# Singles, pairs and the last step: how collected steps are finished in a sequence-and-experts kernel

## The chip, the cores and the metric

The kernel runs on one core of a Trainium2 chip. The metric is the device time of the program in microseconds (us), lower is better; each version is run several times and the median counts. The core has a matrix engine (TensorE, PE in the profile; PEld is its weight load), a vector engine (VectorE, DVE), a scalar engine (ScalarE, ACT), a general engine (GpSimd, POOL) that here mostly issues gathers and scatters, and a queue engine (SyncE, SP) that only issues transfers. ACT and POOL issue transfers too; 16 DMA engines carry them all.

## The reference, cut to what matters

Two sequences (B = 2) of 4096 tokens of width 512 go through two blocks, each followed by a layer normalization of input plus result.

```python
# first block: a matrix W that learns from token to token
pred = W @ k + b;  g = 2.0 / d_h * (pred - v)
W = W - LR * outer(g, k);  b = b - LR * g;  out = W @ q + b
x = layernorm(x + out)
# second block: a shared expert, and 2 of 8 routed experts per token
shared = silu(X @ sW1 + sb1) @ sW2 + sb2
logits = einsum('btd,ed->bte', X, routing_W) + expert_bias
top_vals, top_idx = top_k(sqrt(softplus(logits)), 2)
routed = sum over the two chosen experts e: top_val * (silu(X @ rW1[e] + rb1[e]) @ rW2[e] + rb2[e])
x = layernorm(x + shared + routed)
```

## The kernel before, in words

**Tiling.** The 4096 tokens are cut into 32 chunks of P = 128 tokens; a step `c` (0 to 31) handles chunk `c` of both sequences. The first block is a recurrence over these steps (`step`, with `prep` and `invert` preparing the next one). The second block follows each step one behind (`shared`, which calls `router`). `router` ranks the 8 experts of each token, marks the `chosen` ones (rank 0 or 1), and counts by small matmuls (`pq`) at which place of its expert's list each token goes; POOL scatters the token's number to that place.

**Routed experts.** Steps 0 to 22 are group a, steps 23 to 30 group b; step 31 is done densely. When a group's tokens are all ranked (`plan`), `routed` runs over tiles of 128 tokens of one expert: gather tokens (`g`) and weights (`wb`), multiply, write the tile's rows to memory (`ge`). Group a's tiles run beside steps 24 to 27 of the recurrence, group b's behind the recurrence.

**Collecting.** `collect` brings a group's steps together again, one collected step `j` after the other: load the step's base rows (`acc`, 512 KB, a pool of 4 buffers; the last two steps of group b are still kept on chip as `x`), gather four z tiles (2 sequences x 2 experts, 2 buffers each), add each z with its weight (L956 on DVE), take mean and variance, then normalize and write to the output (`finish`). `fetch(j + 1)` issues the transfers of the next step a little at a time while step `j` is added. With `squares` on, ACT sums the squares into a z tile that has been used (L965), and ACT scales (L927); with it off, DVE takes the statistics (L970, L971) and scales (L930).

**finish.** It takes a small DVE operation on the variance (L915 or L917), a square root on ACT (L918), a reciprocal on DVE (L920, then L922), and for each sequence a scale, then the output transfer on ACT's queue (L932). It is a generator: its first piece ends behind the square root, and each further piece is the scale and output of one step. Steps are finished in pairs (`p = j % 2`): the square root is taken once for two steps, and the pieces are run from inside the next steps, ahead of the products named in `finish_at`.

**Order.** PE and DVE run in the order of the program text; that order comes from `interleave`, which always advances the part whose done share of its stated amount is smallest (a `yield` gives the amount done). ACT's and POOL's orders are laid by the framework. Group a is collected in parts: beside steps 28 to 31 with amounts 16, 16, 16 and 8 (about 3.5, 4, 4 and 2 collected steps), the rest beside group b's tiles and the shared work of step 31. Group b is collected beside the dense work of step 31 (`dense`: for each expert `pd` matmuls, Silu on ACT, `pyd` matmuls, added to x by L721 on DVE; at the end layer normalization and output).

Of the kernel before, what the change touches and what calls it, by code (L numbers as in the profile page):

```python
# [42 lines left out]
BF16 = mybir.dt.bfloat16  # L43
I32 = mybir.dt.int32
AF = mybir.ActivationFunctionType
ALU = mybir.AluOpType
AX = mybir.AxisListType

P = 128
# [5 lines left out]
K = 2  # L55
# [51 lines left out]
def postln_block(ctx: ExitStack, tc: tile.TileContext, x, xT, thK, thV, thQ, w0, b0, masks, blk,  # L107
                 unit, order, rw, eb, w1s, b1s, w2s, b2s, b2e, wcat, out):
    nc = tc.nc
    B, S, D = x.shape  # L110
    NCH = S // P
    DC = D // P
    E = rw.shape[1]
# [20 lines left out]
    sm = ctx.enter_context(tc.tile_pool(name="sm", bufs=2))  # L134
# [137 lines left out]
    groups, of_step = [], {}  # L272
# [239 lines left out]
    def router(c, lg):  # L512
        def small(tag, shape=(P, B, E), bufs=1):
            return sm.tile(list(shape), F32, tag=tag, name=f"{tag}_{c}", bufs=bufs)


        u = small("u")
        nc.vector.scalar_tensor_tensor(u, lg, -1.0, lg, ALU.mult, ALU.min)
        nc.scalar.activation(u, u, AF.Exp)
        yield  # L520
        w = small("w")
        nc.vector.tensor_scalar(w, u, 1.0, None, ALU.add)
        lnw = small("lnw")
        nc.scalar.activation(lnw, w, AF.Ln)

        rank = small("rank")
        full = [P, B, E, E]
        other = lg[:, :, None, :].broadcast_to(full)
        own = lg[:, :, :, None].broadcast_to(full)
        gt = small("gt", full)  # L530
        nc.vector.tensor_tensor(gt, other, own, ALU.is_gt)
        eq = small("eq", full)
        nc.vector.tensor_tensor(eq, other, own, ALU.is_equal)
        nc.vector.tensor_tensor(eq, eq, lower[:, None].broadcast_to(full), ALU.mult)
        nc.vector.tensor_tensor(gt, gt, eq, ALU.add)
        nc.vector.tensor_reduce(rank, gt, AX.X, ALU.add)
        yield
        wm = small("wm")
        nc.vector.tensor_scalar(wm, w, -1.0, None, ALU.add)
        z = small("z")  # L540
        nc.vector.tensor_scalar(z, wm, 0.0, None, ALU.is_equal)
        nc.vector.tensor_tensor(lnw, lnw, z, ALU.add)
        nc.vector.tensor_tensor(wm, wm, z, ALU.add)
        nc.vector.reciprocal(wm, wm)
        nc.vector.tensor_tensor(lnw, lnw, wm, ALU.mult)
        nc.vector.tensor_tensor(lnw, lnw, u, ALU.mult)
        act = small("act")
        nc.vector.scalar_tensor_tensor(act, lg, 0.0, lnw, ALU.max, ALU.add)
        nc.scalar.activation(act, act, AF.Sqrt)
        if c not in of_step:  # L550

            nc.vector.scalar_tensor_tensor(act, rank, K - 0.5, act, ALU.is_lt, ALU.mult)
            yield act
            return

        gr = of_step[c]
        j = c - gr.c0
        chosen = sm.tile([P, B, E], BF16, tag="chosen", name=f"chosen_{c}")
        nc.vector.tensor_scalar(chosen, rank, K - 0.5, None, ALU.is_lt)
        sel = small("sel", (P, B, K, E))  # L560
        full = [P, B, K, E]
        nc.vector.tensor_tensor(sel, rank[:, :, None, :].broadcast_to(full),
                                kk[:, None, :, :].broadcast_to(full), ALU.is_equal)
        yield

        ps = ps_f.tile([P, 2, B, E], F32, tag="pf", name=f"pq_{c}")
        for s in range(B):
            nc.tensor.matmul(ps[:, 0, s], before, chosen[:, s], start=True, stop=(s == 0))
            for r in range(s):
                nc.tensor.matmul(ps[:, 0, s], ones16, chosen[:, r], start=False,  # L570
                                 stop=(r == s - 1))
        for s in range(B):
            nc.tensor.matmul(ps[:, 1, 0], ones16, chosen[:, s], start=(s == 0),
                             stop=(s == B - 1))
        yield
        place = small("place")
        nc.vector.tensor_tensor(place, ps[:, 0],
                                gr.next[:, None, :].broadcast_to([P, B, E]), ALU.add)
        nc.vector.tensor_tensor(gr.next, ps[:, 1, 0], gr.next, ALU.add)
        for what, to in ((place, gr.row), (act, gr.cw)):  # L580
            v = small("selv", (P, B, K, E))
            nc.vector.tensor_tensor(v, sel, what[:, :, None, :].broadcast_to(full), ALU.mult)
            nc.vector.tensor_reduce(to[:, j], v, AX.X, ALU.add)
        ri = sm.tile([P, B, K], I32, tag="ri", name=f"ri_{c}")
        nc.vector.tensor_copy(ri, gr.row[:, j])  # L585
        for s in range(B):
            for k in range(K):
                nc.gpsimd.indirect_dma_start(  # L588
                    out=gr.tables[s * K + k],
                    out_offset=bass.IndirectOffsetOnAxis(ap=ri[:, s, k:k + 1], axis=0),  # L590
                    in_=code[:, j * B + s:j * B + s + 1], in_offset=None,
                    bounds_check=E * gr.cap - 1, oob_is_err=False)
# [287 lines left out]
                weights(k + NW)  # L880
            yield 2.0

    squares, finish_at = [True], [(2, 3)]

    def collect(gr):

# [22 lines left out]
                    z.append(t)  # L909
                    yield  # L910

        def finish(parts, mean, var, on_scalar):

            if on_scalar:
                nc.vector.tensor_scalar(var, var, 1.0 / D, EPS, ALU.mult, ALU.add)  # L915
            else:
                nc.vector.tensor_scalar(var, var, EPS, None, ALU.add)  # L917
            nc.scalar.activation(var, var, AF.Sqrt)  # L918
            yield
            nc.vector.reciprocal(var, var)  # L920
            if on_scalar:
                nc.vector.tensor_tensor(mean, mean, var, ALU.mult)  # L922
            for p, (c, acc) in enumerate(parts):
                for s in range(B):
                    m, v = mean[:, p, s:s + 1], var[:, p, s:s + 1]
                    if on_scalar:
                        nc.scalar.activation(acc[:, s, :], acc[:, s, :], AF.Identity,  # L927
                                             bias=m, scale=v)
                    else:
                        nc.vector.tensor_scalar(acc[:, s, :], acc[:, s, :], m, v,  # L930
                                                ALU.subtract, ALU.mult)
                nc.scalar.dma_start(out=out[:, c * P:(c + 1) * P, :].rearrange("s p d -> p s d"),  # L932
                                    in_=acc)
                yield

        for _ in fetch(0):
            pass
        yield 2.0
        done = iter(())
        for j in range(gr.n):  # L940
            c = gr.c0 + j
            ahead = fetch(j + 1)
            acc, z = got.pop(j)
            p = j % 2
            if p == 0:
                on_scalar, parts = squares[0], []
                two = sm.tile([P, 2, 2, B], F32, tag="fmv", name=f"fmv_{c}")
            mv = two[:, :, p]
            mean, var = mv[:, 0], mv[:, 1]
            parts.append((c, acc))  # L950

            for i in range(B * K):
                s, k = i // K, i % K
                if i in finish_at[0]:
                    next(done, None)
                nc.vector.scalar_tensor_tensor(  # L956
                    acc[:, s, :], z[i], gr.cw[:, j, s, k:k + 1], acc[:, s, :], ALU.mult, ALU.add,
                    accum_out=mean[:, s:s + 1] if on_scalar and k == K - 1 else None)
                next(ahead, None)
                yield 0.9  # L960
            if on_scalar:

                nc.vector.tensor_scalar(mean, mean, -1.0 / D, None, ALU.mult)
                for s in range(B):
                    nc.scalar.activation(z[s * K], acc[:, s, :], AF.Square,  # L965
                                         bias=mean[:, s:s + 1], accum_out=var[:, s:s + 1])
            else:
                for s in range(B):
                    st = sm.tile([P, 6], F32, tag="fst", name=f"fst_{c}_{s}")
                    nc.vector.bn_stats(st, acc[:, s, :])  # L970
                    nc.vector.bn_aggr(mv[:, :, s], st)  # L971
            if p == 1 or j == gr.n - 1:
                for _ in done:
                    pass
                done = finish(parts, two[:, 0, 0:p + 1], two[:, 1, 0:p + 1], on_scalar)
            yield 0.4
        for _ in done:
            pass
# [32 lines left out]
        if c == NCH - 2:  # L1011
            dense_weights(2)
    dense_weights(1 + B + 2)
    squares[0], finish_at[0] = False, (1, 3)
    interleave([(b.tiles * TILE, tiles[1]), (60.0, shared(NCH - 1)),
                ((a.n - sum(COLLECTED.values())) * COLLECT, collects[0])])
    squares[0] = True
    dense_weights(E - len(dense_w))
    interleave([(DENSE, dense(NCH - 1)), (b.n * COLLECT, collects[1])])


def _masks(np):
# [66 lines left out]
```

## Time and profile before

| what | us |
|---|---|
| median of 3 runs | 2638.32 |
| lowest and highest | 2638.26, 2647.33 |
| the profiled execution | 2633.89 |
| its span | 2632.1 |
| square roots of finishing (L918) | 16 passes, 0.205 each |
| table loads ahead of them | 9, 1.283 each |
| scales on ACT (L927), on DVE (L930) | 0.80, 0.54 each |
| gathers of z (L905), POOL's part | 1.01 each |

The profile is one execution. A timeline row gives start and length in us, the engine, the line of the kernel, the operation, what it writes and reads, and in brackets how long the engine stood idle just before it and what ended that wait. `x6` means that six such instructions were merged. `ACTq` and `SPq` are the issue of transfers, not their landing.

### The profile page before, as it was taken

To read this page: it belongs to the slowest core of one execution; us is meant where nothing else is said; L and a number is where in the kernel's file an instruction comes from. 1 tells how busy PE (TensorE), PEld (TensorE's weight loads), DVE (VectorE), ACT (ScalarE), POOL (GpSimd) and SP (SyncE) were. 2 spreads that over 40 slices of the span, in tenths; PEclk is the share of its full clock that TensorE was granted. 3 is DMA by queue.
4 is the path that set the end of the run, shared out by engine and by line. 5 is a ranking of instruction groups with operands and counts; after the bars stand their busy time and mean duration, and the time that the engine had idled before them with its cause. 6 is when DMAs were issued, how large, how long until landed. Compare 5 with 4: busy or idle time off the path is not lost.

```text
span 2632.1 us, 30914 instructions
## 1 busy us (share of the span) xinstructions
PE 2541.5 (97%) x10289; PEld 1642.1 (62%) x10289; DVE 1363.9 (52%) x3993; ACT 723.8 (27%) x1453; POOL 935.0 (36%) x796
## 2 busy tenths in 40 slices
PE   8999999999999999999999999999999999889897
PEld 6666666666666666666665676666767655446664
DVE  2566665565666655666666224223242466553345
ACT  1222222222222222222221232322323233334236
POOL 0223232223232322232324333333333334446654
PEclk9999999999999999999999999999999999989998
DMA  5122222222222222222223343353433456667777
GB/s 185 48 80 59 74 58 66 69 58 58 67 71 74 58 64 71 58 58 63 76 80 130 123 96 105 122 141 109 113 109 109 113 126 169 186 208 224 268 237 245
DMA packets 257647, 291.36 MB, mean 111 GB/s; under 512 B 158269, under 2 KB 171805, under 8 KB 253905
## 3 DMA queue, kind: packets, MB, share of 16 engines
q1 hardware_dynamic: 200624, 165.72, 22.1%
q0 software_dynamic: 48432, 107.42, 14.5%
q10 hardware_dynamic: 8432, 16.25, 1.6%
q8 instruction: 82, 1.34, 0.2%
q14 instruction: 77, 0.62, 0.1%
HBM read 344.38 MB, written 99.65 MB: 169 GB/s over the span
## 4 chain that ended last, share of the span: by engine, by line
PE 85%; issue 5%; DMA 4%; DVE 3%; POOL 2%; ACT 1%; SPq 0%; POOLq 0%; ACTq 0%; DVEq 0%
PE pkq L330 16%; PE pye L857 8%; PE po L449 8%; PE pr L433 8%; PE pr L438 8%; PE phe L846 8%; PE pw L493 8%; PE ph L621 4%; PE py L661 4%; PE pa L343 4%; PE pe L475 2%; PE po L487 2%; PE pg L837 2%; PE pz L414 2%; DMA wb<-wcat_in,widx 1%
## 5 line engine op out<-in xcount | busy, mean ns | idle before, releaser
L375 DVE SCALAR_TENSOR_TENSOR X<-L,X 128x31 f32<-128x31 f32 (+22 forms) x1472 | 409.0, 327 | 27.5 <-DMA L<-dL 10.5
L846 PEld LDWEIGHTS phe<-gT,wb 128*128 128x128 f32 x2208 | 269.7, 194 | 61.9 <-issue 58.9
L588 POOL DMA_INDIRECT gt<-code,ri x124 | 127.3, 1027 | 504.0 <-DVE ri L585 475.4
L860 DVE TENSOR_TENSOR o<-pye,wb 128x512 f32<-128x512 f32 x138 | 95.4, 692 | 400.8 <-PE pye L857 390.0
L857 PE MATMUL pye<-wb,he 128*128 128x512 f32 x552 | 268.7, 609 | 18.8 <-ACT he L850 11.9
L846 PE MATMUL phe<-gT,wb 128*128 128x128 f32 x2208 | 272.9, 277 | 7.0 <-DMA wb<-wcat_in,widx 5.6
L493 PE MATMUL pw<-R,K 128*128 128x512 f32 x496 | 240.6, 608 | 12.7 <-DVE x L488 7.9
L330 PE MATMUL pkq<-xT,thK 128*128 128x256 f32 x1024 | 242.8, 381 | 7.2 <-DMA thK<-thK_in 7.2
L828 POOL DMA_INDIRECT wb<-wcat_in,widx x138 | 144.8, 1049 | 286.2 <-DVE o L860 158.4
L330 PE MATMUL pkq<-xT,thQ 128*128 128x256 f32 x1024 | 244.9, 383 | 1.0 <-DVE Z L416 1.0
L330 PEld LDWEIGHTS pkq<-xT,thK 128*128 128x128 f32 x1024 | 195.0, 191 | 80.1 <-issue 59.3
L449 PE MATMUL po<-W,kq 128*128 128x512 f32 x512 | 242.6, 596 | 1.0 <-DVE K L471 1.0
L433 PE MATMUL pr<-thV,xT 128*128 128x512 f32 x512 | 240.7, 593 | 0.0
L438 PE MATMUL pr<-W,kq 128*128 128x512 f32 x512 | 240.2, 592 | 0.0
L330 PEld LDWEIGHTS pkq<-xT,thQ 128*128 128x128 f32 x1024 | 190.2, 191 | 46.9 <-issue 24.9
L483 POOL PARTITION_ALL_REDUCE ar<-R x23 | 141.6, 6158 | 206.4 <-issue 186.7
L850 ACT ACTIVATE he<-phe,wb 128x128 f32<-128x128 f32 x276 | 86.6, 364 | 436.5 <-PE phe L846 376.9
L337 ACT COPY kq<-pkq 128x256 f32<-128x256 f32 x256 | 82.8, 375 | 433.2 <-PE pkq L330 433.2
L494 DVE TENSOR_TENSOR W<-pw,W 128x512 f32<-128x512 f32 x248 | 168.5, 689 | 63.3 <-PE pw L493 59.6
L822 POOL DMA_INDIRECT g<-gy,gidx x138 | 139.8, 1013 | 153.4 <-PE pg L837 120.7
L493 PEld LDWEIGHTS pw<-R,K 128*128 128x128 f32 x496 | 91.4, 192 | 136.3 <-issue 97.8
L857 PEld LDWEIGHTS pye<-wb,he 128*128 128x128 f32 x552 | 98.5, 190 | 124.8 <-issue 90.8
(214 smaller groups left out, 3394.9 us busy)
## 6 DMA issues: line engine op xcount, KB each, us to landing
ge<-o SPq DMA_DIRECT2D x138, 256.0 KB
xT<-xT_in SPq DMA_DIRECT2D x32, 512.0 KB
x<-x_in SPq DMA_DIRECT2D x32, 512.0 KB
L<-dL SPq DMA_DIRECT2D x128, 128.0 KB
gy<-x SPq DMA_DIRECT2D x31, 512.0 KB
gb<-x SPq DMA_DIRECT2D x29, 512.0 KB
y_out<-acc ACTq DMA_DIRECT2D x29, 512.0 KB
dT_K<-kq SPq DMA_DIRECT2D x92, 128.0 KB
```

What stands on the lines that cost most here:

```text
L330: nc.tensor.matmul(ps[:, i].rearrange("p s t -> p (s t)"), th[:, dc, (ec + i) * P:(ec + i + 1) * P], xt[:, dc].rearrange("p s t -> p (s t) ...
L375: nc.vector.scalar_tensor_tensor(X[:, h, j + 1:], L[:, j + 1:, j], X[:, h, j:j + 1], X[:, h, j + 1:], ALU.mult, ALU.add)
L433: nc.tensor.matmul(ps, xt[:, dc, s, :], nthV_sb[:, dc, :], start=(dc == 0), stop=False)
L438: nc.tensor.matmul(ps, KQ[:, ec, s, 0, :], W[s][:, ec, :], start=False, stop=(ec == DC - 1))
L449: nc.tensor.matmul(ps, KQ[:, ec, s, 1, :], W[s][:, ec, :], start=(ec == 0), stop=False)
L483: nc.gpsimd.partition_all_reduce(ar, R, P, bass_isa.ReduceOp.add)
L493: nc.tensor.matmul(ps, K[s][:, ec, :], F[s], start=True, stop=True)
L494: nc.vector.tensor_tensor(W[s][:, ec, :], ps, W[s][:, ec, :], ALU.add)
L822: nc.gpsimd.indirect_dma_start(out=g_t[k], out_offset=None, in_=gr.y, in_offset=bass.IndirectOffsetOnAxis(ap=gr.gidx[:, k:k + 1], axis=0), ...
L828: nc.gpsimd.indirect_dma_start(out=wbuf[k % NW], out_offset=None, in_=wcat, in_offset=bass.IndirectOffsetOnAxis(ap=gr.widx[:, k:k + 1], ax ...
L846: nc.tensor.matmul(ps[:, hc, :], w[:, dc * HF + hc * P:dc * HF + (hc + 1) * P], t[:, dc, :], start=(dc == 0), stop=(dc == DC - 1))
L857: nc.tensor.matmul(ps, h[:, hc, :], w[:, O2 + hc * D:O2 + (hc + 1) * D], start=(hc == 0), stop=(hc == HC - 1))
```

## The change

It has four parts. Collected steps are finished in pairs only once `paired` is set, which happens behind the recurrence; before that each step is finished alone, and so are the last two steps of each group. The very last collected step is scaled half on DVE and half on ACT, with one output transfer on SP's and one on ACT's queue. `chosen` is computed right behind `rank` and no longer behind the activation's chain. The stated amount of group b's collecting is 1.1 times what it was.

```diff
@@ router
         nc.vector.tensor_reduce(rank, gt, AX.X, ALU.add)
+        if c in of_step:
+            chosen = sm.tile([P, B, E], BF16, tag="chosen", name=f"chosen_{c}")
+            nc.vector.tensor_scalar(chosen, rank, K - 0.5, None, ALU.is_lt)
         yield
...
         j = c - gr.c0
-        chosen = sm.tile([P, B, E], BF16, tag="chosen", name=f"chosen_{c}")
-        nc.vector.tensor_scalar(chosen, rank, K - 0.5, None, ALU.is_lt)
         sel = small("sel", (P, B, K, E))
@@ collect
-    squares, finish_at = [True], [(2, 3)]
+    squares, finish_at, paired = [True], [(2, 3)], [False]
...
-        def finish(parts, mean, var, on_scalar):
+        def finish(parts, mean, var, on_scalar, final):
...
                     m, v = mean[:, p, s:s + 1], var[:, p, s:s + 1]
-                    if on_scalar:
+                    if final and s == 0:
+
+                        nc.vector.tensor_scalar(acc[:, s, :], acc[:, s, :], v, m,
+                                                ALU.mult, ALU.add)
+                        nc.sync.dma_start(out=out[s, c * P:(c + 1) * P, :], in_=acc[:, s, :])
+                    elif on_scalar:
...
-                nc.scalar.dma_start(out=out[:, c * P:(c + 1) * P, :].rearrange("s p d -> p s d"),
-                                    in_=acc)
+                if final:
+                    nc.scalar.dma_start(out=out[1, c * P:(c + 1) * P, :], in_=acc[:, 1, :])
+                else:
+                    nc.scalar.dma_start(
+                        out=out[:, c * P:(c + 1) * P, :].rearrange("s p d -> p s d"), in_=acc)
...
-        done = iter(())
+        done, parts = iter(()), []
...
-            p = j % 2
+            p = 0 if len(parts) != 1 else 1
             if p == 0:
-                on_scalar, parts = squares[0], []
+                on_scalar = squares[0]
...
-            if p == 1 or j == gr.n - 1:
+            if p == 1 or not paired[0] or j >= gr.n - 2:
                 for _ in done:
                     pass
-                done = finish(parts, two[:, 0, 0:p + 1], two[:, 1, 0:p + 1], on_scalar)
+                done = finish(parts, two[:, 0, 0:p + 1], two[:, 1, 0:p + 1], on_scalar,
+                              gr is groups[-1] and j == gr.n - 1)
+                parts = []
@@ behind the recurrence
-    squares[0], finish_at[0] = False, (1, 3)
+    squares[0], finish_at[0], paired[0] = False, (1, 3), True
...
-    interleave([(DENSE, dense(NCH - 1)), (b.n * COLLECT, collects[1])])
+    interleave([(DENSE, dense(NCH - 1)), (1.1 * b.n * COLLECT, collects[1])])
```

## The prediction, made before the changed kernel ran

> **What bounds the kernel now.** I read the page first. TensorE is busy nearly all the time, so an edit pays only where PE stands still or in the stretch behind its last matmul.
>
> ```profile
> PE 2541.5 (97%) x10289; PEld 1642.1 (62%) x10289; DVE 1363.9 (52%) x3993; ACT 723.8 (27%) x1453; POOL 935.0 (36%) x796
> ```
>
> Collecting begins in step 28, so I then took the busy time of each engine over steps 28, 29 and 30 (from one step's first `pr` matmul to the next).
>
> ```profile
> 2094.21:2158.82 64.61, 62.30 (x223) 37.91 (x222) 45.40 (x140) 20.09 (x42) 30.43 (x30) 1.00 0.51 116
> 2158.82:2224.45 65.63, 62.56 (x223) 38.06 (x222) 44.84 (x146) 24.22 (x51) 29.25 (x29) 1.00 0.64 170
> 2224.45:2298.89 74.44, 64.58 (x222) 38.91 (x221) 44.89 (x146) 24.21 (x51) 29.19 (x29) 0.93 0.69 198
> ```
>
> Columns: stretch, length, busy us of PE, PEld, DVE, ACT, POOL, granted clock, DMA share, GB/s. Step 30 has the work of step 29 and takes 8.8 us more, at a clock of 0.93. The timeline shows why:
>
> ```profile
> 2264.67 0.38 ACTq L932 DMA_DIRECT2D y_out<-acc  x1
> ...
> 2269.63 0.75 POOL L898 DMA_DIRECT2D acc<-gb  x1 [0.31 <-issue]
> ...
> 2281.26 0.75 DVE L956 SCALAR_TENSOR_TENSOR acc<-z,cw,acc 128x512 f32<-128x512 f32 x1 [8.47 <-DMA acc<-gb]
> ...
> 2286.11 5.21 PE L493 MATMUL pw<-R,K 128*128 128x512 f32 x6 [7.91 <-DVE x L488]
> ```
>
> I count the L956 rows: 2281.26 is the first product of collected step 11. Its base rows `acc` use the buffer of step 7 (four buffers). Step 7 is the second of pair (6,7), so it is scaled only inside step 9, at 2263.84, and written at 2264.67; POOL can issue the load at 2269.63, and it lands at 2281.24. DVE, in program order, stands 8.47 us, with the eviction L488 behind it; PE stands 7.91 us. Its next six `pw` matmuls take 5.21 us, the clock being 0.70 from 2285 to 2295.
>
> Last the end of the run:
>
> ```profile
> 2603.90 1.02 POOL L905 DMA_INDIRECT z<-ge,sidx  x1 [0.30 <-issue]
> ...
> 2609.11 0.79 DVE L956 SCALAR_TENSOR_TENSOR x<-z,cw,x 128x512 f32<-128x512 f32 x1 [4.23 <-DMA z<-ge,sidx]
> ...
> 2612.23 2.84 PE L718 MATMUL pyd<-wb,hd 128*128 128x512 f32 x6 [1.62 <-ACT hd L710]
> ...
> 2614.28 0.74 DVE L721 SCALAR_TENSOR_TENSOR x<-pyd,act,x 128x512 f32<-128x512 f32 x1
> ...
> 2628.12 0.38 ACTq L932 DMA_DIRECT2D y_out<-x  x1
> ```
>
> PE ends near 2615; 17 us of DVE, ACT and output follow, up to 2632.1.
>
> **Singles in the recurrence.** Walking the yields, steps 0 to 12 now finish one by one, (13,14) to (19,20) in pairs, 21 and 22 alone. The output of step 7 then leaves at the last product of step 8: the scale that now stands at 2254.58 (step 6's) becomes step 7's, with its write at 2256.1 instead of 2264.67. The write took about 4.4 us until POOL was released (2264.67 to 2269.1), so the load can go near 2261 and has 11.8 us until DVE wants it at 2272.8, against 11.6 measured. The stall goes. What is late next: the gathers of step 11, issued at 2267.01 and 2268.31 in the same queue ahead of that load, so landed before 2281. Bounds for step 30: 4 us if they hold DVE, 9.8 if it falls to step 28's 64.61. I take step 29's length, nearest because it has the same finishes: **-8.8**. Step 29 has a smaller such wait (1.7 us on `acc`) and is 1.0 longer than step 28: **-1.0** (0 to -1.0).
>
> Added: sqrt passes rise from 16 to 24, seven of them here, each with three small DVE rows (0.16, 0.17, 0.16). 7 x 0.5 = 3.5 us over four steps in which DVE has some 20 us idle per step: nothing. The new wait is L920 on ACT's sqrt; queued behind it is the step's last product, then evictions. The sqrt falls between the products at 2263.38 and 2264.68, where ACT does `act`'s sqrt at 2263.72 anyway; if that cover is gone it costs one table load, 1.28.
>
> A rule speaks against this part. The sqrt's table loads number 9 in 16 passes, the first at 2369.3: none inside the recurrence, and a load takes 1283 ns. The Trainium skill, ScalarE: Activation LUTs, "What ACT_TABLE_LOAD costs", puts a switch at that plus about 1.38 us of drain, 2.66 in all. Seven passes, there and back, would by it be 37 us of ACT; by the rows 0 to 18. The rows also show no drain (load 2563.76 + 1.28, sqrt at 2565.05), so I take them. ACT idles 41 us per step: even the rule's price would meet PE only if it held a `kq` copy beyond the 6.51 us that such copies wait for PE.
>
> **Chosen behind the ranks.** PE waits for `chosen` twice only: 3.00 us at 1400.03 and 2.90 at 2317.98. At the first, ranks end at 1398.24; `chosen` takes 0.17, so `pq` starts near 1398.5: -1.5, and nothing else holds the `pkq` matmuls behind it. At the second, ranks end at 2314.9, but the `py` matmuls behind `pq` need the second Silu, which ends at 2318.42: only -0.5. **-2.0**, bounds 0 and -5.9. No other queue is touched.
>
> **Behind the recurrence.** PE waits 5.13 us for the first routed tokens, issued 2343.08, with DMA share 1.01 from 2349 to 2361. Two 0.5 MB outputs (2344.68, 2349.02) are in flight; one of them now leaves in step 31 before. 0.5 MB at the 402 GB/s of that stretch is 1.3 us; by halves between queues **-0.7** (0 to -1.4). The tile loop has six sqrt passes before and after: nothing.
>
> **The final stage.** With 1.1 the collecting is placed before more of the dense work: the last dense half is now behind everything that collecting does on DVE. The stage runs in rounds of two steps: z lands, products, squares (which give z free), gather, landing. Rounds, by first products of steps 0, 2, 4, 6: 14.1, 15.5, 13.1 us. Now one dense eviction less (0.7) stands in each: three rounds, step 6 starts 2.1 earlier. Behind it: products of step 6 with two dense evictions, 4.9; ACT's scales (1.6) and squares (1.8) until L915, 7.5; two more scales, a table load and the sqrt, 10.6; last product, eviction and first layernorm, 14.2; ACT scale, squares and small rows, 17.8; DVE scale 0.55, last eviction, layernorm and ACT scale, 21.8; output 3.0: 24.8, against 23.0 now (2609.11 to 2632.1). 1.8 - 2.1 = **-0.3**. Bounds: -4 if ACT takes the sqrts first, +5 if each of its passes queues behind scales.
>
> The output price: two 0.5 MB writes end 4.0 us after the last issue. The skill's DMA: Bandwidth & Descriptors, "Anatomy of one DMA", has 2.0 us fixed plus bytes at 436 GB/s, 2.6 for 0.25 MB. Halving the row's moved part from about 2 us to 1 gives 3.0; by the rule the sum would be 0.4 better.
>
> **The sum.** -8.8 - 1.0 - 2.0 - 0.7 - 0.3 = -12.8 us. The profiled execution ran 2633.89 (span 2632.1), and would run 2621.1; the median of the runs is 4.4 above it, so I forecast 2638.3 - 12.8 = **2625.5**.
>
> **Rivals.**
> - *The next transfer is late.* The gathers of step 11 hold DVE for half the stall. For: DMA share 0.97 from 2265 to 2275. Against: they stand ahead of the load. Step 30 gains 4: -8.0 in all, 2630.
> - *Everything helps.* Step 30 falls to 64.61 (-9.8), `chosen` gives 4 because the clock's dip behind the wait goes too (eight `pkq` at 1400.16 take 3.59 us, at 1407.02 1.89), tail -4, tokens -1.4, step 29 -1.0: -20, 2618. For: the clock rows. Against: ACT has 15 us of work in the last 20.
> - *The final stage turns against it: slower.* DVE now waits for z ahead of evictions for which PE needs a bank. If gathers land like the base load, in 11.6 us instead of 4.5, a round is 4.4 + 2.5 + 11.6 = 18.5 us; step 6 starts at 2566.4 + 55.5 = 2621.9, 12.8 late, and with the 1.8 of the tail and -12.5 elsewhere this gives +2.1: 2640. It decides from rounds of about 18 us; the longest now is 15.5. For: DMA share near 0.9 there; against: no round came near.
>
> **Chances.** Forecast 0.45, late transfer 0.21, everything 0.22, final stage 0.12. Differences below 0.5% are about what a measurement of this kernel can't tell from none; faster by more is below 2625.1. Just under half of the forecast's share (0.22), all of the third case and 0.02 of the second lie there: 0.46. Slower by more (above 2651.5) takes 0.10: most of the last case, since longer landings have no upper row. 0.44 is left. Forecast's own range 2621 to 2631; with the others 2614 to 2641.
>
> **What would show it.** Right: step 30 near 65 us at clock 1.00, no wait of DVE on `acc<-gb` over 2 us; `pq` without a wait at the first place and a wait on the Silu at the second; 24 sqrt passes; a final 0.25 MB output. Wrong: DVE held in step 30 by `z`, or PE held in the dense stage by L721.

## The result, and the profile after

| | us, or ratio to the kernel before |
|---|---|
| before, median of 20 runs | 2635.48 |
| after, median of 20 runs | 2643.90 |
| ratio, 95% interval | 1.0026 [1.0017, 1.0034] |
| after again, 12 runs beside 35 of before | 1.0019 [1.0008, 1.0030] |
| profiled execution of after, its span | 2636.67, 2634.9 |

The forecast was 2625.5, 12.8 below the median of before that the prediction had (2638.3, three runs; twenty give 2635.48). The change made the kernel 0.2 to 0.3% slower. That is inside the 0.5% which the prediction called no difference, but with twenty runs a side it is told from none, and it has the other sign. The profiled execution of after is a quick one, 7.2 us under the median of its runs.

The same windows as before, steps 28, 29 and 30 of after (stretch, length, busy us of PE, PEld, DVE, ACT, POOL, clock, DMA share, GB/s):

```profile
2094.70:2160.20 65.50, 62.55 (x222) 37.99 (x221) 46.84 (x144) 20.20 (x44) 30.21 (x30) 1.00 0.50 121
2160.20:2225.90 65.70, 62.61 (x223) 38.11 (x222) 43.94 (x152) 24.78 (x53) 29.75 (x29) 1.00 0.56 172
2225.90:2293.70 67.80, 62.53 (x222) 38.04 (x221) 43.33 (x152) 24.60 (x53) 27.51 (x28) 1.00 0.66 204
```

Step 30 is 6.6 us shorter by these windows (6.8 by the exact cuts below) and its clock is whole again: in this execution the stall is nearly gone. The time must be lost later. I cut each execution at the first `pr` of steps 30 and 31, at the first `pg` (group b's first tile), at the first `pd` (dense work) and at the end of the span:

| version (profiled us) | step 30 | step 31 to first tile | tile loop | rest |
|---|---|---|---|---|
| before (2633.89) | 74.6 | 56.0 | 203.1 | 74.2 |
| after (2636.67) | 67.8 | 57.8 | 209.5 | 73.9 |
| after again (2651.66, highest of its runs) | 73.1 | 60.4 | 214.0 | 74.0 |

The first execution of after against before: -6.8, +1.8, +6.4 and -0.3, with +1.6 up to step 30 (0.9 of it in step 28). The sum, 2.8 with rounding, is the difference of the two profiled times. The gain is made in step 30 and lost in the tile loop, in which I had counted no change.

The timeline of after shows where PE waits there. First POOL in step 31, and the PE row that needs its work (`pc` turns the gathered `codes` into the numbers of the tokens):

```profile
2331.83 0.76 POOL L899 DMA_DIRECT2D acc<-gb  x1 [7.02 <-DMA y_out<-acc]
2332.90 0.99 POOL L769 DMA_INDIRECT codes<-gt,r  x1 [0.30 <-issue]
...
2340.95 2.52 PE L811 MATMUL pc<-ident,codes 39*128 39x39 f32 x8 [7.74 <-DMA codes<-gt,r]
```

The base load of collected step 14 needs the buffer of step 10, whose output has not landed. POOL stands 7 us at it, and the four `codes` gathers, which need nothing from it, stand behind. In before this load came behind `codes`, `wb` and `g` and stood 9.5 us with no `codes` gather behind it:

```profile
2337.73 0.96 POOL L768 DMA_INDIRECT codes<-gt,r  x1 [0.30 <-issue]
...
2357.73 0.76 POOL L898 DMA_DIRECT2D acc<-gb  x1 [9.52 <-DMA y_out<-acc]
```

Second, in the tile loop of after (`phe` are the first matmuls of a tile with its expert's weights `wb`):

```profile
2411.38 1.04 POOL L829 DMA_INDIRECT wb<-wcat_in,widx  x1 [3.51 <-issue]
2412.46 0.38 ACTq L941 DMA_DIRECT2D y_out<-acc  x1
...
2421.05 3.44 PE L847 MATMUL phe<-gT,wb 128*128 128x128 f32 x16 [2.10 <-DMA wb<-wcat_in,widx]
...
2423.70 0.75 POOL L899 DMA_DIRECT2D acc<-gb  x1 [8.64 <-DMA y_out<-acc]
2424.75 1.05 POOL L829 DMA_INDIRECT wb<-wcat_in,widx  x1 [0.30 <-issue]
...
2428.13 2.02 PE L847 MATMUL phe<-gT,wb 128*128 128x128 f32 x16 [1.20 <-DMA wb<-wcat_in,widx]
```

Again a base load (step 17) waits for an output, 8.64 us, with weight gathers behind it, and PE waits for `wb` twice. Only the second of these waits can come from the held load. The gather for which the `phe` at 2421.05 wait was issued at 2411.38, ahead of it, and landed more than nine us later; why it took so long was not tested. Behind this wait the sixteen `phe` take 3.44 us instead of 2.02. The waits of PE in the tile loop of before (2343 to 2558, first two rows) and of after (2340 to 2560): total, times, longest.

```profile
PE phe L846 <- DMA wb<-wcat_in,widx: 5.6, 4, 2.4
PE pg L837 <- DMA g<-gy,gidx: 5.1, 1, 5.1
...
PE phe L847 <- DMA wb<-wcat_in,widx: 13.3, 7, 3.3
PE pc L811 <- DMA codes<-gt,r: 7.7, 1, 7.7
```

The wait for `codes` stands mostly in place of the wait for the first tokens `g`; the waits for weights are 7.7 us more.

### The profile page after: what moved, and what is told of

It is laid out like the page before. It is cut to its first block, busy times and chain, and to the rows that moved or that the text cites. A ratio compares the mean times of both kernels' runs of the same rounds, so it can differ in the third digit from the quotient of the medians.

```text
span 2634.9 us, 30962 instructions
## 1 busy us (share of the span) xinstructions
PE 2541.3 (96%) x10289; PEld 1642.4 (62%) x10289; DVE 1362.7 (52%) x4015; ACT 726.9 (28%) x1466; POOL 933.8 (35%) x796
## 5 line engine op out<-in xcount | busy, mean ns | idle before, releaser
L330 PEld LDWEIGHTS pkq<-xT,thK 128*128 128x128 f32 x1024 | 195.2, 192 | 80.4 <-issue 59.6
```

The lines of the kernel that those rows point to most:

```text
L330: nc.tensor.matmul(ps[:, i].rearrange("p s t -> p (s t)"), th[:, dc, (ec + i) * P:(ec + i + 1) * P], xt[:, dc].rearrange("p s t -> p (s t) ...
```

## The experiments

Each ratio is to the kernel before, run beside that version, with its 95% interval. There before took 2635 to 2638 us, but 2650 beside h1_sync14, h_cut12, i_e1_sync and i_bef_sync, so their stage times are compared among themselves first. Each version has 11 or 12 runs (e2_singles and k3_late 6, m1_before_late 5), and the stage times are of one execution. Theory A took several forms; each expectation says which.

### One part at a time

*e1_chosen*: before, `chosen` moved. *e2_singles*: before, singles in the recurrence. *e3_final*: before, only the final stage (last two steps of group b alone, last step split, 1.1). *e4_ten*: the changed kernel, with singles only up to step 9.

```diff
# e1_chosen is the router part of the change alone
# e2_singles: the changed kernel, chosen put back, amount b.n * COLLECT, never final
-            if p == 1 or not paired[0] or j >= gr.n - 2:
+            if p == 1 or not paired[0] or j == gr.n - 1:
# e3_final: the changed kernel, chosen put back
-    squares, finish_at, paired = [True], [(2, 3)], [False]
+    squares, finish_at, paired = [True], [(2, 3)], [True]
-            if p == 1 or not paired[0] or j >= gr.n - 2:
+            if p == 1 or j >= gr.n - 2 + (gr is not groups[-1]):
# e4_ten, against the changed kernel
-            if p == 1 or not paired[0] or j >= gr.n - 2:
+            if p == 1 or (not paired[0] and j < 10) or j >= gr.n - 2:
```

> Only the marking of the chosen experts is moved; all else is the kernel before. Theory A (POOL's order): no change of POOL's order by this part, so 0 to -2 us against the kernel before; pq without a wait in step 24, and py waiting for the Silu in step 31 instead. Rival B (the final stage costs): the same. Rival C (the marking itself disturbs DVE's order): slower by 3 us or more.

> Only the single finishing of collected steps in the recurrence; marking, last two steps, the split of the last step and the 1.1 are as before. Theory A: the whole loss is here. Step 30 is 6 to 7 us shorter, step 31 with the plan about 6 longer (POOL stands 5 us or more on a load of base rows ahead of the gathers of codes, PE waits 5 us or more for codes), the tile loop about 6 longer; in all +3 to +9 us against the kernel before. Rival B: -6 us, since only step 30's gain is left.

> Only the final stage: the last two steps of group b single, the last one split over two engines, the amount times 1.1; marking and recurrence as before. Theory A: 0 (-2 to +2 us), the stage behind the last tile 74 us as before. Rival B: +5 us or more, PE held by L721 or by the Silu in the dense stage.

> The changed kernel, but single finishing only up to collected step 9; from step 10 on pairs as before, so that POOL's order at the plan and in the tile loop is that of the kernel before. Theory A: step 30 keeps its 6 to 7 us, codes come without a wait of PE, the tile loop is as long as before: -5 to -9 us against the kernel before. Rival B: the loss of the final stage stays, so 0 to +5 us against the kernel before.

| | ratio | step 30 | step 31 to first tile | tile loop | rest |
|---|---|---|---|---|---|
| e1_chosen | 1.0019 [1.0008, 1.0030] | 78.4 | 56.4 | 201.7 | 76.2 |
| e2_singles | 1.0051 [1.0034, 1.0067] | 71.1 | 61.6 | 212.7 | 75.7 |
| e3_final | 0.9997 [0.9987, 1.0008] | 73.0 | 59.6 | 197.8 | 77.0 |
| e4_ten | 0.9982 [0.9969, 0.9995] | 71.0 | 56.0 | 198.2 | 76.9 |
| e4_ten again | 0.9983 [0.9973, 0.9994] | 70.8 | 54.7 | 198.7 | 77.5 |

Singles cause the loss, and in step 31 and the tile loop. Three singles fewer turn the change into a gain. Two surprises: `chosen` alone costs time, in steps 29 (68.1 for 65.6) and 30; and the singles alone lose more than the whole change does. The second I cannot explain.

### Why moving chosen alone cost time

With `chosen` moved, the planner (the part of the framework that lays the orders of ACT and POOL) orders ACT differently at two places: an output (steps 3 and 7) comes behind a sum of squares instead of ahead of it, and POOL's next base load one gather later. Nothing else moves but DVE's small operations. The timeline of e1_chosen, in step 30:

```profile
2268.67 0.33 SPq L691 DMA_DIRECT2D thQ<-wcat_in  x1
2268.87 0.38 ACTq L933 DMA_DIRECT2D y_out<-acc  x1
2270.43 0.33 SPq L691 DMA_DIRECT2D wd<-wcat_in  x1
...
2282.35 0.75 POOL L899 DMA_DIRECT2D acc<-gb  x1 [8.86 <-DMA y_out<-acc]
...
2288.12 0.75 DVE L957 SCALAR_TENSOR_TENSOR acc<-z,cw,acc 128x512 f32<-128x512 f32 x1 [12.39 <-DMA acc<-gb]
```

In before this output was issued at 2264.67 and had landed some 4.4 us later. Here it goes 0.2 us behind a 1 MB weight load, and POOL sees it landed only at 2282, 13 us later. Two runs send the outputs of steps 3 and 7 from SP's queue, which gives POOL's order of before back:

```diff
-                nc.scalar.dma_start(out=out[:, c * P:(c + 1) * P, :].rearrange(...
+                (nc.sync if c in (3, 7) else nc.scalar).dma_start(out=out[:, c * P:(c + 1) * P, :].rearrange(...
```

> Chosen moved alone, as in the run that was 5.8 slower than before, but the outputs of collected steps 3 and 7 are issued on SP's queue, so that they no longer stand behind a sum of squares on ACT; POOL's order is then that of the kernel before. Theory A (moving chosen cost time only because the planner put these two outputs and with them two base loads one place later): steps 29 and 30 fall from 68.1 and 78.4 to 65.6 and at most 74.6, whole time 2633 to 2635, no slower than before. Rival C (chosen's new place itself delays DVE or PE): steps 29 and 30 stay above 67 and 77, whole time about 2640.

> Control: the kernel before with the outputs of collected steps 3 and 7 issued on SP's queue, chosen where it was. Both theories: within 3 us of the kernel before (2632 to 2638), step 30 between 70 and 75; the difference between this and the run with chosen moved is then what chosen itself does, 0 to -2 by my sum.

Measured: with `chosen` moved 0.9988 [0.9976, 1.0000], the control 0.9993 [0.9981, 1.0005]. Steps 29 and 30 of the first are 65.3 and 73.9. So the cost was the place of two outputs, and `chosen` itself is worth some 0.05%, 1.3 us, with intervals that overlap. A second pair says the same from e4_ten, taking its `chosen` back:

> Singles up to collected step 9 and the final stage as in the changed kernel, chosen where it was before. POOL's order is the same as with chosen moved, ACT's differs in one copy. Theory A (chosen alone gives 0 to 2 us where the outputs keep their places): 0 to 2 us slower than the same version with chosen moved, ratio to before 0.998 to 0.9995. Rival C (chosen's place costs time of itself): faster than that version by 2 us or more, ratio below 0.9978.

0.9994 [0.9981, 1.0007], against 0.9982 and 0.9983 with `chosen` moved: 3 us by the middle values, with intervals that overlap. `chosen` gives between nothing and 3 us.

### What costs time in step 31 and the tile loop

```diff
# h1_sync14: the changed kernel; j_after_14_17: "j in (14, 17)"
-                queue = nc.sync if gr is groups[-1] else nc.gpsimd
+                queue = nc.sync if gr is groups[-1] or j == 14 else nc.gpsimd
# h_cut12: singles up to step 11; h_cut11: up to 10; h_cut14: up to 13
+            if p == 1 or (not paired[0] and j < 12) or j >= gr.n - 2:
# j_cut12_14: h_cut12 with the first edit
```

> The changed kernel with one instruction moved: the base load of collected step 14, which waits for an output ahead of the four codes gathers on POOL, is issued on SP's queue; every other engine's order stays. Theory A (the loss is the codes gathers held behind that waiting load): the 7.7 us wait of pc on codes falls to about 3, the piece of step 31 behind its first pr falls from 57.8 to 56, and the tile loop from 209.5 towards 200, since its first weights and tokens start earlier; whole time about 2634, 9 below the changed kernel. Rival B (the loss is the other order of weight and token gathers inside the tile loop, laid by the planner): only the 2 us in step 31 go, the tile loop stays at 208 or more, whole time about 2641.

> The changed kernel with singles up to collected step 11 and pairs from 12 on: step 10 is still finished alone, so the waiting load of step 14 stands ahead of codes as in the changed kernel, but the order of gathers inside the tile loop is that of the faster version with singles up to step 9. Theory A (held codes): slow, about 2641 to 2644, tile loop 207 or more. Rival B (order in the tile loop): fast, about 2632, tile loop about 199, with only 2 us lost in step 31.

> The changed kernel once more, beside the three that follow, since times of different calls differ by more than the effects asked for. All theories: 1.0017 to 1.0034 of the kernel before.

> The changed kernel with two base loads on SP's queue: that of collected step 14 (it holds the four codes gathers) and that of step 17 (it stood 8.64 us on POOL at 2423.70 with the weight gathers of the next routed tiles behind it); all other orders are those of the changed kernel. Theory A (the loss is POOL held by base loads that wait for an output): the tiles that began at 2421 and 2428 no longer take 6.5 and 7.0 us but 4.2 to 4.8, the time falls 5 to 9 us below the changed kernel, ratio to before 0.9990 to 1.0005. Rival B (the order of the gathers themselves, or DMA engines that are full): the tiles stay slow or others get slow, the time stays within 2 us of the changed kernel. Rival D (SP's stores of expert rows are held by the moved load and with them the tile loop): slower than the changed kernel.

> Singles up to collected step 11 (pairs even-odd in the tile loop, as before) with the base load of step 14 on SP's queue, so that it doesn't hold codes. Theory A: step 30 stays near 68, the piece of step 31 ahead of the first tile falls by 2 to 5 us, and the whole is the fastest so far, ratio to before 0.996 to 0.998. Rival B: no faster than the version with singles up to step 9, ratio 0.998 or more.

> The changed kernel with step 13 finished alone too, so that the pairs behind the recurrence are (14,15), (16,17), (18,19), (20,21). Theory E (the pairing odd-even is what costs in the tile loop): tiles 10 and 11 of group b take 4.2 and 4.8 us again, the tile loop under 205, ratio to before 0.997 to 0.9995. Rival F (the more steps are finished alone, the later the tile loop): as the changed kernel or slower, ratio 1.0015 or more.

> The changed kernel with singles only up to step 10, so that the pairs are (11,12), (13,14) and so on, odd-even as in the changed kernel. Theory E: slow, tiles 10 and 11 take 6 to 7 us, ratio 1.001 to 1.003. Rival F: between the versions with singles up to 9 and 11, ratio 0.998 to 0.999.

A tile's length is the distance between first `phe` matmuls (tiles counted from 0):

| version | singles up to | ratio | step 31 to first tile | tile loop | tiles 10, 11 |
|---|---|---|---|---|---|
| before | none | 1 | 56.0 | 203.1 | 4.2, 4.8 |
| e4_ten | 9 | 0.9982 | 56.0 | 198.2 | 4.2, 4.8 |
| h_cut11 | 10 | 1.0018 [1.0006, 1.0030] | 60.4 | 208.2 | 6.8, 7.0 |
| h_cut12 | 11 | 0.9979 [0.9965, 0.9994] | 57.8 | 208.9 | 4.2, 4.8 |
| j_cut12_14 | 11 | 0.9992 [0.9980, 1.0004] | 59.9 | 204.6 | 4.2, 4.8 |
| after | 12 | 1.0026 | 57.8 | 209.5 | 6.5, 7.1 |
| h1_sync14 | 12 | 1.0003 [0.9988, 1.0018] | 60.2 | 215.2 | 6.7, 7.0 |
| j_after_14_17 | 12 | 1.0013 [1.0002, 1.0023] | 61.2 | 211.3 | 5.8, 4.3 |
| h_cut14 | 13 | 1.0016 [0.9998, 1.0033] | 61.0 | 209.5 | 6.9, 4.3 |

The tile loops have to be read with one correction. In five of the twenty executions (before, h_cut12, h1_sync14, i_e1_sync, i_bef_sync) ACT starts a Silu of the loop 2.4 to 4.5 us behind the end of its matmuls, once to three times, and the profile names no instruction or transfer of the kernel as what ended its wait (`remote`). Before, and h_cut12:

```profile
2498.80 0.63 ACT L850 ACTIVATE he<-phe,wb 128x128 f32<-128x128 f32 x2 [5.83 <-remote]
...
2497.61 0.63 ACT L851 ACTIVATE he<-phe,wb 128x128 f32<-128x128 f32 x2 [7.32 <-remote]
```

In before tile 26 is 8.7 us long with this, in h_cut12 10.4, and tile 14 there 7.4; in e4_ten, which has no such row, both take 4.2. Without it, an estimate from these tile lengths, the loop of before would be some 199 us, and that of h_cut12 too. With these two and the fifteen executions that have no such row, the loops go with the ratios: 198 to 205 us for no singles and for singles up to 9 and 11, and 208 to 214 for 10, 12 and 13. So the change costs the loop about 11 us, more than the 6.4 of the first two executions.

The `codes` gathers are not shown to be the main loss. In h_cut12 POOL waits 6.89 us ahead of them, and it is fast; taking that wait away in j_cut12_14 gave nothing that can be seen. In h1_sync14 the wait of `pc` falls to 0.7, but PE waits 9.18 us for the first token gather instead, and the tile loop, with three late Silus in it, cannot be told from that of the changed kernel. Its ratio is 0.2% under that of the changed kernel, so the wait may cost something; j_after_14_17, which has the same edit and one more, doesn't repeat that size. The second held load is real in the trace but small: with the load of step 17 off POOL, tile 11 falls from 7.0 to 4.3 as expected, tile 10 from 6.9 to 5.8 only, and tile 12 rises from 4.3 to 5.5. Some 2.5 of 5 us come back; the time falls by 0.06%, which is within the noise. That tile 10 stays slow fits the rows of after: the gather for which PE waits at its end was issued ahead of the load. In j_after_14_17 PE waits 1.41 us for that gather, with no held load on POOL.

Singles up to 10 and up to 12 give the slow tiles, up to 9 and 11 don't, so I took odd-even pairs for the cause. That falls with h_cut14, which pairs even-odd and has a slow tile 10 and a loop of 209.5. What is shown is narrower: which gathers and loads stand ahead of which on POOL differs with each cut, and the ratio does not go with the number of singles.

### What made the stall of step 30

In after, DVE waits at the same place for something else, and PE behind it:

```profile
2263.30 0.75 POOL L899 DMA_DIRECT2D acc<-gb  x1 [0.62 <-ACT z L974]
...
2278.04 0.75 DVE L965 SCALAR_TENSOR_TENSOR acc<-z,cw,acc 128x512 f32<-128x512 f32 x1 [3.42 <-DMA z<-ge,sidx]
...
2283.13 3.04 PE L493 MATMUL pw<-R,K 128*128 128x512 f32 x6 [3.08 <-DVE x L488]
```

And in the second execution of after:

```profile
2283.47 0.75 DVE L965 SCALAR_TENSOR_TENSOR acc<-z,cw,acc 128x512 f32<-128x512 f32 x1 [6.05 <-DMA z<-ge,sidx]
...
2288.39 5.49 PE L493 MATMUL pw<-R,K 128*128 128x512 f32 x6 [5.54 <-DVE x L488]
```

The base load has come, the `z` gathers haven't, and the wait differs from execution to execution. Over four executions with the changed order up to here (after, after again, h1_sync14, j_after_14_17) step 30 took 67.8, 73.1, 69.1 and 71.0, 4.3 less than before on average. All twelve with the early output and the weight loads in place took 66.9 to 73.7, 70.1 on average; four with the output where before has it (before, e3_final, i_e1_sync, i_bef_sync) took 73.0 to 74.6, 73.7 on average. So the early output is worth some 4 us. I suspected what all these transfers share. Two 1 MB loads of dense weights are issued here too; in the timeline of before:

```profile
2265.74 0.33 SPq L690 DMA_DIRECT2D thQ<-wcat_in  x1
2267.50 0.33 SPq L690 DMA_DIRECT2D wd<-wcat_in  x1
```

They are wanted only behind the tile loop. A one-column write by DVE, which the load overwrites, holds each back to the end of step 30 or 31; beside these two small rows of DVE only SP's order changes. *k3_late* has it on e4_ten, *m1_before_late* on before (pairs, `chosen` and final stage as they were), *m2_after_late* on the changed kernel.

```diff
+            if e in (1, 5):
+                nc.vector.memset(t[:, 0:1], 0.0)
             nc.sync.dma_start(out=t, in_=wcat[e * P:(e + 1) * P, 0:OB1])
```

> Singles up to collected step 9, else the changed kernel, and two of the 1 MB loads of dense weights wait for a one-column write of DVE at the end of step 30 and of step 31, so that they are no longer issued at 2268 and 2270 beside the z gathers and outputs of step 30. Theory A (these loads make z late): DVE's wait for z in step 30 falls from 5.2 to under 2 us, step 30 from 71 to 66 to 67, ratio to before 0.9965 to 0.998. Rival B (z is late because of the outputs and base loads of collecting itself): step 30 stays at 69 or more, ratio 0.998 or more.

> The kernel before, with the two 1 MB weight loads held back to the end of step 30 and of step 31 as in the fastest version; pairs as before. Theory A (the loads made the stall): the base load issued near 2269.6 lands in about 5 us instead of 11.6, DVE's wait on it falls from 8.5 to under 3 us, step 30 from 74.6 to 66 to 69, ratio to before 0.996 to 0.998. Rival G (the late output of step 7 made it, as predicted): step 30 stays above 72, ratio above 0.9985.

> The changed kernel with the same two loads held back. Theory A: step 30 at 66 to 67, but the tile loop keeps its slow tiles 10 and 11, so that it loses to the version with singles up to step 9 and held-back loads (0.9945) by 6 to 10 us: ratio to before 0.997 to 1.000. Rival H (the slow tiles too come from these loads): as fast as that version, below 0.996.

| | median | ratio | step 30 | step 31 to first tile | tile loop | rest |
|---|---|---|---|---|---|---|
| k3_late | 2625.16 | 0.9945 [0.9926, 0.9965] | 66.5 | 56.8 | 203.3 | 74.6 |
| m1_before_late | 2624.74 | 0.9962 [0.9949, 0.9976] | 65.6 | 54.7 | 198.9 | 75.0 |
| m2_after_late | 2636.17 | 1.0005 [0.9996, 1.0014] | 65.7 | 56.0 | 210.2 | 74.6 |

The window of step 30 and the timeline of m1_before_late:

```profile
2224.19:2289.78 65.59, 62.56 (x222) 38.08 (x222) 44.68 (x146) 24.21 (x51) 29.71 (x29) 1.00 0.65 177
```

```profile
2264.46 0.38 ACTq L934 DMA_DIRECT2D y_out<-acc  x1
...
2269.49 0.75 POOL L900 DMA_DIRECT2D acc<-gb  x1 [0.17 <-issue]
...
2274.00 0.75 DVE L958 SCALAR_TENSOR_TENSOR acc<-z,cw,acc 128x512 f32<-128x512 f32 x1 [1.30 <-DMA acc<-gb]
...
2279.18 3.04 PE L493 MATMUL pw<-R,K 128*128 128x512 f32 x6 [1.07 <-DVE x L488]
```

The reader should lay this beside the four rows of before in the prediction. Output and base load are issued at the same times to 0.2 us (2264.67 and 2269.63 there) behind the same pair. The load lands in 4.5 us instead of 11.6, and the stall is gone with no output moved. In the three executions with the weight loads held back PE waits 1.1 us at this place; in the seventeen others 2.4 to 11.8. So the late output of step 7 makes no stall by itself: the stall needs the weight loads, one or both. While they are in flight, an earlier output takes about half of it away, and what is late next holds DVE.

m2_after_late shows what the change does once that is gone: beside m1_before_late, step 30 is equal, and the tile loop 11.3 longer, with tiles 10 and 11 again at 6.4 and 7.1 (4.5 of the 11.3) and POOL held again:

```profile
2420.21 0.75 POOL L901 DMA_DIRECT2D acc<-gb  x1 [8.62 <-DMA y_out<-acc]
```

So the slow tiles don't come from the weight loads. The fastest versions are k3_late and m1_before_late, whose intervals overlap; m1_before_late has nothing of the change in it.

## Why the prediction was wrong, point by point

**Singles, step 30: -8.8 forecast.** The stall on `acc` went as the prediction said, and "what is late next: the gathers of step 11" was what came. It held DVE 3.4 and 6.1 us. The value for this, 4, stood in the first rival, and the executions give some 4. The failed choice is "I take step 29's length". Behind it lies a cause that I had not asked for: I found that the load lands late (11.6 us) and shortened the way to it, without asking why 512 KB took so long with two 1 MB loads issued around it.

**Step 29: -1.0 forecast.** 65.7 in after, 65.6 before: nothing. The finishing rows on DVE, put at nothing, have a small price in step 28: it takes 65.5 us in all fourteen executions with singles and 64.6 in the six without, and in after PE waits 0.5 us there for a row of DVE.

**The square roots.** Right. There are 24 passes, table loads rise from 9 to 10, and the first is at 2394.2, behind the recurrence: the rule of 37 us on ACT had no case here.

**Chosen: -2.0 forecast.** At the first place PE's wait fell from 3.00 to 1.31, and the next `pr` rows came 3 us earlier (33.4 us behind those at 1371.88 in before, 30.5 in after). Within 100 us it was given back: PE waits 1.83 us for `g` at 1447.54, and the clock is 0.94 instead of 1.00 from 1444 to 1473. The `pr` rows at 1503.56 in before stand 131.7 us behind the same rows, in after 131.8. At the second place the Silu held PE, as worked out:

```profile
2310.33 0.19 PE L569 MATMUL pq<-chosen,before 128*128 128x8 bf16 x2 [0.33 <-DVE chosen L539]
...
2313.64 1.13 PE L662 MATMUL py<-w,h 128*128 128x512 f32 x2 [2.08 <-ACT h L641]
```

"No other queue is touched" was wrong: alone, the move changed ACT's and POOL's order at two places and cost 5.8 us by the medians. Together with singles up to step 9 (e4_ten, g1_ten_old) POOL's order is the same with and without it.

**Behind the recurrence: -0.7 forecast, +8.2 measured** in the first execution (+1.8 and +6.4), and more where no late Silu stretches the tile loop of before: m2_after_late against m1_before_late is 1.3 and 11.3. This is the step of the sum that failed. I counted the one output that leaves earlier, and for the tile loop the square roots: "nothing". A buffer that comes free at another time moves its base load in POOL's order, and in that queue stand the gathers that feed PE. I named the queues for the step that I moved, but not for the loads that wait on it.

**The final stage: -0.3 forecast.** 73.9 for 74.2, but the exact hit is luck. Counted from the first `pd`, step 6 starts 1.2 us earlier (2.1 forecast), and from there to the end it takes 23.9 us for 23.0 (1.8 longer forecast): both terms came at about half. PE waited 3.64 us for the Silu at 2619.54, behind ACT's scales. The last output, 0.25 MB, ends 3.2 us after its issue at 2631.68, near the 3.0 counted; the rule set beside it, with 2.6, is given for transfers that POOL issues, and this one goes from SP. The slower rival had its place here and was wrong about it: the slowing came in the tile loop. Changed alone, e3_final, it is 0.9997.

**Left open.** Why singles alone (1.0051) lose more than singles with the other parts (1.0026 and 1.0019); which of the exchanged gathers costs the rest of the 11 us in the tile loop, and whether the outputs issued beside them slow them, as the weight loads slow the base load in step 30; what makes those Silus late; and which of the two weight loads does the harm in step 30.

## What to carry to other kernels

When a transfer is late, first ask why it took so long, not how to start it earlier: look for large loads of low urgency issued beside it, and hold those back. Where a planner lays the order of a queue, an edit that frees a buffer at another time reorders that queue; before you cost it at nothing, list what stands behind the load that waits for the buffer, and who waits for that.

## What the runs showed of the hardware

The same 512 KB transfer at the same time of the same step took 4.5 us (m1_before_late) or 11.6 us (before), with a DMA share of 0.87 and 0.97 over the ten us in which it was issued: its price was set by what was in flight with it. An output issued 0.2 us behind a 1 MB load was seen to land 13 us later (e1_chosen), and one issued 1 us ahead of such a load in some 4.4 (before). And a long stall costs more than its idle time. In the twenty executions the same six `pw` of step 30 took 3.0 us behind waits of up to 2.4 us (four executions) and 4.3 to 5.5 us behind waits of 4.3 us and more (ten). Between 3.0 and 3.9 us it fell either way: 3.0 us in two, 4.2 to 5.5 in four, and behind the same wait of 3.87 us 3.03 in h_cut12 and 5.49 in j_after_14_17.
